# Interleaved halves of the second expert weights in a mixture-of-experts loop

## Chip, cores and metric

The kernel runs on one core of one Trainium2 chip. The metric is device time in microseconds from launch to end; the figure of a kernel is the median of its runs. Before the change that is 1061.54 us (three runs, 1061.35 to 1062.29).

## What is computed

A graph layer and a transformer block work on 625 nodes of 768 features. The graph layer (two attention convolutions over 20,000 edges with self-loops, layer norms, residual products) and the attention with 12 heads take roughly the first 630 us of the span and are not touched. The change is in the last part, a mixture of 8 experts of which each node uses one:

```python
gate_logits = h2 @ Wg                      # h2: layer norm of x, [625, 768]
w, sel = jax.lax.top_k(gate_logits, 1)     # K = 1: the softmax weight is 1
hid = relu(einsum('nd,edf->enf', h2, W1) + b1[:, None, :])   # W1: [8, 768, 3072]
y = einsum('enf,efd->end', hid, W2) + b2[:, None, :]         # W2: [8, 3072, 768]
out = x + (the y of the expert that the node chose)
```

All of it is in float32. An expert's two matrices have 9.4 MB each; they are read from DRAM once for every expert that has nodes.

## The kernel before, in words

**Steps.** The nodes are sorted by expert, and a loop written for the device (L1364) runs over *steps*. A step treats M = 128, 64 or 32 rows of one expert; one branch of the loop body is compiled for each size. One step of 128 rows (A) runs ahead of the loop. In the profiled run the loop's nine steps have 64, 128, 64, 32, 128, 64, 32, 64 and 32 rows. Steps of one expert follow each other without a reload.

**Pieces and halves.** Each matrix lies in SBUF as three pieces: `w1[c]` holds all 768 rows and 1024 columns of the first weights as [128, 6, 1024], `w2[c]` holds 1024 rows of the second weights as eight blocks of 128 rows, [128, 8, 768]. There is one buffer for each piece. `load_piece` (L1034) fills a piece with two DMAs of 1.5 MB on SyncE's queue, a *half* each: for first weights three of the six row blocks, for second weights blocks 0 to 3 and blocks 4 to 7. `w1[2]` has buffers ahead (`load_ahead`, L1081), from which ScalarE copies it (`from_ahead`, L1085), so that this piece is asked for one step sooner.

**Chunks.** `step` (L1088) puts P = 128 / M groups of columns side by side in the array, so that each matmul uses M columns of it. It goes over the hidden features in n chunks. `into(c)` (L1099) multiplies the rows by a chunk of the first weights, `turn(c)` (L1111) transposes the result and applies bias and relu, and `out_of(c)` (L1122) multiplies by the second weights and adds up over all chunks in two PSUM banks (`py[i]`, i the half of the output columns). For M = 128 there are six chunks of 512 hidden features, so chunk c uses one half of piece c // 2. For M = 64 and 32 there are three chunks, each a whole piece; group g of a 64-row chunk works on blocks 4g to 4g + 3, group g of a 32-row chunk on blocks 2g and 2g + 1. K is the number of blocks to a group: 4, 4 and 2. In the trace each float32 matmul is two instructions.

**Order.** Inside a step TensorE's order is written out by hand: the first `into`s, then `turn`s and `out_of`s. `out_of` goes over k (blocks of a group) outside and i inside, in the last chunk over i outside, so that VectorE can add one half of the output (L1184) while the other is computed. SyncE's order is fixed as well (`load_expert`, L1069): `w1[0]`, `w1[1]`, the bias, `w2[0]`, the two buffers ahead, `w2[1]`, `w2[2]`. These loads are issued while the step before still computes, each as soon as the last reader of its destination is done; where the next step has the same expert, they are issued with a false condition and move nothing. GpSimd's queue carries the gathers of rows and the final scatter of each step.

Of the kernel before, what the change touches and what calls it, by code (L numbers as in the profile page):

```python
# [25 lines left out]
KD = D // 128  # L26
# [21 lines left out]
FC = 1024  # L48
# [14 lines left out]
def gnn_moe_kernel(ctx: ExitStack, tc: tile.TileContext, p, out):  # L63
    nc = tc.nc
# [26 lines left out]
    def halves(name, w, k, n):  # L91

        r = k // 2 * 128
        return [wload(f"{name}{i}", k // 2, n,
                      w[i * r:(i + 1) * r, :].rearrange("(k p) n -> p k n", p=128))
                for i in range(2)]
# [51 lines left out]
    with tc.tile_pool(name="gnn", bufs=1) as gp:  # L148
        C = gp.tile([R, T, N], F32, name="C")
# [30 lines left out]
        with tc.tile_pool(name="oneh", bufs=12) as op_, \  # L180
# [15 lines left out]
            w1 = halves("w1", p["L0_gnn_W1"], KD, HC)  # L196
# [253 lines left out]
            with tc.If(ok == 0):  # L450

                nc.vector.memset(C, 0.0)
                for a in range(0, EJ, PART):
                    clear()
                    for q in range(a, a + PART):
                        g, j = q // GJ, q % GJ
                        ohs = step(past[:, g, j:j + 1], True)
                        ohd = target(N, dst[:, g, j:j + 1], upper[:, g, j:j + 1])
                        for t in range(T):
                            nc.tensor.matmul(cps[:, t, :SH + 1], ohd[:, cols(t)], ohs, start=False,  # L460
                                             stop=False, skip_group_check=True)
# [14 lines left out]
        with tc.tile_pool(name="gw", bufs=2, reuse_waits="tile") as gw, \  # L476
# [68 lines left out]
            w2 = halves("w2", p["L0_gnn_W2"], KH, D)  # L545
# [148 lines left out]
    with tc.tile_pool(name="att", bufs=1, reuse_waits="tile") as a1, \  # L694
# [11 lines left out]
        def head_weights(name, w, which=(0, 1)):  # L706
            got = []
            for i in which:
                t_ = wp.tile([128, 3072], F32, tag="w", name=f"{name}{i}")
                v_ = t_[:, :KD * 384].rearrange("p (k n) -> p k n", k=KD)  # L710
                for k in range(KD):
                    nc.sync.dma_start(
                        v_[:, k, :].rearrange("p (h s) -> p h s", h=6),
                        w[6 * i:6 * i + 6, k * 128:(k + 1) * 128, :].rearrange("h p s -> p h s"))
                got.append(v_)
            return got
# [51 lines left out]
        w = head_weights("L0_ffn_Wv", p["L0_ffn_Wv"])  # L768
        for t in range(T):
            for i in range(2):  # L770
                pp = ps.tile([128, 512], F32, tag="p1", name="pv")
                for c in range(KD):
                    nc.tensor.matmul(pp[:R, :384], hT[:, c, cols(t)], w[i][:, c, :],
                                     start=(c == 0), stop=(c == KD - 1))
# [212 lines left out]
        for i in range(len(units) + 2):  # L987
            if i < len(units):
                j, t = units[i]
# [9 lines left out]
            if i >= 2:  # L999
                j, t = units[i - 2]  # L1000
# [22 lines left out]
    W1, W2, b2 = p["L0_ffn_W1"], p["L0_ffn_W2"], p["L0_ffn_b2"]  # L1023
    w1, w2 = [None] * NFC, [None] * NFC
# [8 lines left out]

    def load_piece(e, l, c, **cond):  # L1034
        if l:
            for k in range(0, FC // 128, 4):
                nc.sync.dma_start(  # L1037
                    w2[c][:, k:k + 4, :],
                    W2[ds(e, 1), c * FC + k * 128:c * FC + (k + 4) * 128, :]
                    .rearrange("o (k p) d -> p (o k) d", p=128), **cond)  # L1040
        else:
            for k in range(0, KD, 3):
                load_half(w1[c][:, k:k + 3, :], e, c, k, **cond)
# [44 lines left out]
    def step(M, xT, bT, rb, after=None):  # L1088
# [3 lines left out]
        P = B // M  # L1092
        C = 512 if P == 1 else FC // P
        n = DF // (C * P)
        K = C // 128
        py = [sp.tile([128, 512], F32, name=f"py{i}", bufs=1) for i in range(2)]
        hb, hbT, copied = {}, {}, []

        def into(c):  # L1099
            ph = sp.tile([128, 512], F32, name="ph")  # L1100
            w, o = (w1[c // 2], (c % 2) * C) if P == 1 else (w1[c], 0)
            for k in range(KD):
                for g in range(P):
                    mm = nc.tensor.matmul(ph[g * M:(g + 1) * M, :C], xT[:, k, :M],  # L1104
                                          w[:, k, o + g * C:o + (g + 1) * C],
                                          start=(k == 0), stop=(k == KD - 1))
            hb[c] = mw.tile([128, 512], F32, name="hb")
            copied.append(nc.vector.tensor_copy(hb[c][:, :C], ph[:, :C]))  # L1108
            return mm

        def turn(c):  # L1111

            tp = sp.tile([128, 4, 128], F32, tag="tp", name="tph")
            for k in range(K):
                nc.tensor.transpose(tp[:, k, :], hb[c][:, k * 128:(k + 1) * 128], ident)  # L1115
            hbT[c] = mw.tile([128, 4, 128], F32, name="hbT", bufs=6)
            for k in range(K):
                for g in range(P):
                    f, r = c * P * K + g * K + k, slice(g * M, (g + 1) * M)
                    nc.scalar.activation(hbT[c][:, k, r], tp[:, k, r], AF.Relu, bias=bT[:, f:f + 1])  # L1120

        def out_of(c):  # L1122
            w, o = (w2[c // 2], (c % 2) * K) if P == 1 else (w2[c], 0)

            order = [(k, i) for k in range(K) for i in range(2)]
            for k, i in sorted(order, key=lambda o: o[1]) if c == n - 1 else order:
                for g in range(P):
                    mm = nc.tensor.matmul(  # L1128
                        py[i][g * M:(g + 1) * M, :384], hbT[c][:, k, g * M:(g + 1) * M],
                        w[:, o + g * K + k, i * 384:(i + 1) * 384],  # L1130
                        start=(c == 0 and k == 0), stop=(c == n - 1 and k == K - 1))
            return mm

        with tc.manual_schedule(engines={PE}):
            into(0)
            begun = into(1)
# [42 lines left out]
        w = 384 * P // 4  # L1179
# [30 lines left out]
    for i, n in ((0, T), (1, TA)):  # L1210
        for s in range(n):
            nc.tensor.matmul(pc[:1, i * E:(i + 1) * E], ones[:, :1], oh[:, s, :], start=(s == 0),
                             stop=(s == n - 1))

    def row8(name, *shape, tag=None):
        return ap.tile([1, *shape], F32, name=name, tag=tag or name)
# [18 lines left out]
    key = row8("key", E)  # L1235
# [91 lines left out]
    w = tabf[:, 2, :NS]  # L1327
# [36 lines left out]
    with tc.For_i(0, n_blk, 1, iteration_sync="reg_based") as i:  # L1364
        w = word(i)
# [50 lines left out]
```

## Time and profile before

| What | Value |
|---|---|
| Median of the runs | 1061.54 us |
| The profiled execution's own time | 1062.57 us |
| Its span, first to last instruction | 1060.6 us |
| TensorE busy | 1003.9 us, 95% of the span |
| VectorE, ScalarE, GpSimd busy | 456.6, 366.6, 57.1 us |
| Moved by DMA | 195.90 MB, mean 185 GB/s |
| Mean granted TensorE clock | 0.988 of full speed |
| `out_of` (L1128): 960 matmul instructions | 191.7 us |
| `into` (L1104) in the loop: 864 matmul instructions | 154.5 us |
| Loads of pieces of expert weights: issues on SyncE's queue | 114, 1.5 MB each |

The page lists the busy time of each engine, the span in 40 slices, the chain of work that ended last, and groups of instructions with their mean length and the idle time before them, together with what ended that idle time. A busy matmul is a modelled figure, since matmuls are pipelined; the spacing of their starts tells more than their lengths. In the chain, a step of TensorE, a wait for a DMA or a step of another engine each stand with start and length; what is on it sets the end. A window gives the busy time of each engine in a stretch, then the granted clock (1.00 is full), the share of time that the 16 DMA engines were busy, and what they moved. In the names, `ew` is a buffer of expert weights, `hbT` the turned hidden rows, `ph` and `py` the PSUM tiles of `into` and `out_of`.

### The profile page before, as it was taken

The numbers are of one execution on the slowest core, as the hardware profiler recorded it, in microseconds if no ns is written. First come the engines' busy times: TensorE is split into PE (matmuls) and PEld (weight loads), VectorE is DVE, ScalarE is ACT, GpSimd is POOL, SyncE is SP. The second block draws the span as 40 slices with busy tenths as digits, with TensorE's granted clock in tenths as the row PEclk, the third lists the DMA queues.
The fourth block names the chain that finished last, engine by engine and source line by source line (L and its number), as shares of the span: only waits on it lengthen the run. The fifth ranks groups of instructions, "written<-read, shape, count | busy, mean of one in ns | idle before, by whom it ended". The sixth has DMA issues, their size and how long they took to land. (4 is left out here: it accounts for less than half of the span.)

```text
span 1060.6 us, 15061 instructions
## 1 busy us (share of the span) xinstructions
PE 1003.9 (95%) x4763; PEld 571.8 (54%) x4764; DVE 456.6 (43%) x1307; ACT 366.6 (35%) x835; POOL 57.1 (5%) x97
## 2 busy tenths in 40 slices
PE   6889999999999999999999999998999989999893
PEld 4455466677555556666665655543454434534341
DVE  7886796385284930565546655011101121011212
ACT  6667554362040111444433401113131333034231
POOL 1200100000000010000000112000000000000000
PEclk9999999999999999999999999999999999999997
DMA  9300400300420266999000759333659986899793
GB/s 284 134 1 1 161 31 0 134 1 15 90 44 1 69 156 139 403 392 372 4 1 4 294 174 338 128 141 127 241 214 393 405 309 261 323 399 398 280 404 122
DMA packets 86195, 195.90 MB, mean 185 GB/s; under 512 B 32429, under 2 KB 34100, under 8 KB 86137
## 3 DMA queue, kind: packets, MB, share of 16 engines
q1 hardware_dynamic: 80617, 177.14, 46.3%
q0 software_dynamic: 5440, 17.86, 4.9%
q8 instruction: 32, 0.52, 0.2%
q10 hardware_dynamic: 80, 0.16, 0.1%
q14 instruction: 26, 0.21, 0.1%
HBM read 253.45 MB, written 38.37 MB: 275 GB/s over the span
## 5 line engine op out<-in xcount | busy, mean ns | idle before, releaser
L1128 PE MATMUL py<-ew,hbT 128*64 128x384 f32 (+2 forms) x960 | 191.7, 502 | 10.6 <-DMA ew<-in_L_ffn_W_dram 10.6
L1104 PE MATMUL ph<-ew,xbT 128*32 128x256 f32 (+2 forms) x864 | 154.5, 491 | 5.0 <-DVE bT L1067 3.9
L1128 PEld LDWEIGHTS py<-ew,hbT 128*64 128x64 f32 (+2 forms) x960 | 90.6, 147 | 93.0 <-issue 58.1
L1120 ACT ACTIVATE hbT<-tph,bT 128x64 f32<-128x64 f32 (+2 forms) x240 | 55.2, 332 | 215.4 <-PE tph L1115 148.6
L1104 PEld LDWEIGHTS ph<-ew,xbT 128*32 128x32 f32 (+2 forms) x864 | 61.7, 133 | 87.1 <-issue 78.8
L1184 DVE TENSOR_TENSOR yo<-yo,py 64x192 f32<-64x192 f32 (+2 forms) x80 | 27.6, 378 | 163.0 <-PE py L1128 162.1
L1108 DVE COPY hb<-ph 128x512 f32<-128x512 f32 (+1 forms) x39 | 24.4, 628 | 149.4 <-PE ph L1104 148.5
L530 PE MATMUL agg<-xl,zT 125*125 125x256 f32 (+1 forms) x300 | 79.8, 417 | 1.3 <-ACT zT L519 1.1
L530 PEld LDWEIGHTS agg<-xl,zT 125*125 125x125 f32 x300 | 54.5, 188 | 19.6 <-ACT zT L519 2.6
L357 PE MATMUL pp<-w,yT 128*125 128x512 f32 x120 | 56.8, 613 | 0.0
L232 ACT ACTIVATE step<-iota,past 125x314 f16<-125x314 f16 x120 | 55.9, 549 | 0.0
L630 PE MATMUL ph<-wr,h1T 128*125 128x384 f32 x160 | 52.8, 486 | 0.0
L592 PE MATMUL ph<-w,h1T 128*125 128x384 f32 x160 | 52.4, 486 | 0.0
L839 ACT ACTIVATE e<-e,nm 125x125 f32<-125x125 f32 (+4 forms) x60 | 36.0, 602 | 39.5 <-DVE nm L836 39.5
L249 PE MATMUL cps<-step,oh 125*125 125x314 f16 x181 | 37.0, 307 | 10.5 <-ACT step L232 4.8
L902 PE MATMUL po<-wpj,aT 128*125 128x384 f32 x120 | 44.3, 499 | 1.2 <-DVE nm L836 0.7
L242 DVE TENSOR_SCALAR oh<-iota,drel,upper 125x125 f16<-125x125 f16 x160 | 41.1, 314 | 2.9 <-PE cps L249 2.8
L167 PE MATMUL ph<-wr,yT 128*125 128x512 f32 x96 | 42.1, 593 | 0.1
L592 PEld LDWEIGHTS ph<-w,h1T 128*125 128x125 f32 x160 | 30.0, 188 | 21.2 <-issue 0.5
L836 DVE CUSTOM_DVE_ANT_0 e<-sc,later 125x125 f32<-125x125 f32 (+4 forms) x60 | 30.7, 543 | 24.1 <-PE sc L830 24.0
L630 PEld LDWEIGHTS ph<-wr,h1T 128*125 128x125 f32 x160 | 29.8, 188 | 20.8
L810 PE MATMUL pq<-hT,L_ffn_Wq 128*128 128x313 f32 (+1 forms) x144 | 40.9, 432 | 0.0
(333 smaller groups left out, 1298.4 us busy)
## 6 DMA issues: line engine op xcount, KB each, us to landing
ew<-in_L_ffn_W_dram SPq DMA_DIRECT2D x114, 1536.0 KB
xr<-zt SPq DMA_DIRECT2D x5, 3076.0 KB
xg<-zt SPq DMA_DIRECT2D x5, 3072.0 KB
ahead<-in_L_ffn_W_dram SPq DMA_DIRECT2D x10, 1536.0 KB
xid<-in_L_ffn_W_dram SPq DMA_DIRECT2D x10, 1536.0 KB
w<-in_L_gnn_W_dram SPq DMA_DIRECT2D x4, 1536.0 KB
wr<-in_L_gnn_Wr_dram SPq DMA_DIRECT2D x4, 1536.0 KB
b2b<-in_L_ffn_b_dram SPq DMA_DIRECT2D x11, 384.0 KB
```

The costliest lines, as they stand in the source:

```text
L167: nc.tensor.matmul(pp[:R, :], yT[:, c, cols(t)], part(wr1, KD, c, i, 512), start=(c == 0), stop=(c == KD - 1))
L232: nc.scalar.activation(o, iota[:, :SH + 1], AF.Sign, bias=at, scale=-1.0)
L242: m = nc.vector.tensor_scalar(o, iota[:, :n], at, weight, op0=OP.is_equal, op1=OP.mult)
L357: nc.tensor.matmul(pp[:R, :], yT[:, c, cols(t)], part(w1, KD, c, i, 512), start=(c == 0), stop=(c == KD - 1))
L530: nc.tensor.matmul(self.agg[:R, c0:c0 + n], zT[:, s, :], xl[:, s, x0:x0 + n], start=(s == 0), stop=(s == T - 1))
L592: nc.tensor.matmul(ph[:R, :384], h1T[:, c, cols(t)], part(w2, KH, c, i, 384), start=(c == 0), stop=(c == KH - 1))
L630: nc.tensor.matmul(ph[:R, :384], h1T[:, k, cols(t)], part(wr2, KH, k, i, 384), start=(k == 0), stop=(k == KH - 1))
L810: nc.tensor.matmul(pp[:, :b - a], w[:, c, c0:c0 + 128], hT[:, c, a:b], start=(c == 0), stop=(c == KD - 1))
L902: mm = nc.tensor.matmul(pp[:R, i, :384], aT[:, c, cols(t)], wpj[i][:, c, :], start=(c == 0), stop=(c == KD - 1))
L1104: mm = nc.tensor.matmul(ph[g * M:(g + 1) * M, :C], xT[:, k, :M], w[:, k, o + g * C:o + (g + 1) * C], start=(k == 0), stop=(k == KD - 1))
L1120: nc.scalar.activation(hbT[c][:, k, r], tp[:, k, r], AF.Relu, bias=bT[:, f:f + 1])
L1128: mm = nc.tensor.matmul(py[i][g * M:(g + 1) * M, :384], hbT[c][:, k, g * M:(g + 1) * M], w[:, o + g * K + k, i * 384:(i + 1) * 384], start ...
```

## The change

A half of a piece of the second weights now holds every other block: the first DMA brings blocks 0, 2, 4 and 6, the second 1, 3, 5 and 7. What uses the halves follows:

- In steps of 128 rows chunk c uses the blocks of the same parity as c: block 2k + c % 2. Its columns of the first weights are then four runs of 128, every other block of 128 columns; the product lands in PSUM as one stretch of 512, as before. The bias columns follow.
- In steps of 64 and 32 rows group g keeps its blocks gK + k. `out_of` goes over the k with even blocks first, then those with odd blocks: 0, 2, 1, 3 for 64 rows and 0, 1 for 32 rows. In the last chunk i stays outside.

```diff
     def load_piece(e, l, c, **cond):
         if l:
-            for k in range(0, FC // 128, 4):
-                nc.sync.dma_start(
-                    w2[c][:, k:k + 4, :],
-                    W2[ds(e, 1), c * FC + k * 128:c * FC + (k + 4) * 128, :]
-                    .rearrange("o (k p) d -> p (o k) d", p=128), **cond)
+            of_e = W2[ds(e, 1), c * FC:(c + 1) * FC, :].rearrange(
+                "o (k two p) d -> two p (o k) d", two=2, p=128)
+            to = w2[c].rearrange("p (k two) d -> two p k d", two=2)
+            for i in range(2):
+                nc.sync.dma_start(to[i], of_e[i], **cond)
...
+        def block(c, g, k):
+            return 2 * k + c % 2 if P == 1 else g * K + k
+
         def into(c):
             ph = sp.tile([128, 512], F32, name="ph")
-            w, o = (w1[c // 2], (c % 2) * C) if P == 1 else (w1[c], 0)
+            if P == 1:
+                w = w1[c // 2].rearrange("p k (j two f) -> p k two j f", two=2, f=128)[:, :, None, c % 2]
+            else:
+                w = w1[c].rearrange("p k (g j f) -> p k g j f", g=P, f=128)
             for k in range(KD):
                 for g in range(P):
-                    mm = nc.tensor.matmul(ph[g * M:(g + 1) * M, :C], xT[:, k, :M],
-                                          w[:, k, o + g * C:o + (g + 1) * C],
-                                          start=(k == 0), stop=(k == KD - 1))
+                    mm = nc.tensor.matmul(
+                        ph[g * M:(g + 1) * M, :C].rearrange("p (j f) -> p j f", f=128),
+                        xT[:, k, :M], w[:, k, g], start=(k == 0), stop=(k == KD - 1))
...
-                    f, r = c * P * K + g * K + k, slice(g * M, (g + 1) * M)
+                    f = block(c, g, k) + (c // 2 if P == 1 else c) * (FC // 128)
+                    r = slice(g * M, (g + 1) * M)
...
         def out_of(c):
-            w, o = (w2[c // 2], (c % 2) * K) if P == 1 else (w2[c], 0)
+            w = w2[c // 2 if P == 1 else c]
-            order = [(k, i) for k in range(K) for i in range(2)]
+            order = [(k, i) for k in sorted(range(K), key=lambda k: block(c, 0, k) % 2)
+                     for i in range(2)]
...
-                        w[:, o + g * K + k, i * 384:(i + 1) * 384],
+                        w[:, block(c, g, k), i * 384:(i + 1) * 384],
```

## The prediction

> **What bounds the kernel now.** I read the page first, for the chain that ended last, then the matmul groups with shapes kept apart, to see whose wait is on that chain.
>
> ```profile
> PE 27%; DMA 5%; issue 0%; DVE 0%; POOLq 0%; DVEq 0%; SPq 0%
> ```
>
> ```profile
> L1128 PE MATMUL py<-ew,hbT 128*32 128x384 f32 x288 | 31.6, 536 | 10.6 <-DMA ew<-in_L_ffn_W_dram 10.6
> ```
>
> TensorE is busy nearly throughout. The only transfers it waits for in the expert loop are second weights, 10.6 us, all in the steps of 32 rows (stationary 128x32); the forms of 64 and 128 rows show none. The chain in order of time says when (start, length, what):
>
> ```profile
> 841.69 1.03 PE ph L1104 x16
> ...
> 842.82 19.33 DMA ew<-in_L_ffn_W_dram
> ...
> 862.29 2.77 PE py L1128 x28
> ...
> 1024.12 20.18 DMA ew<-in_L_ffn_W_dram
> ...
> 1044.44 4.49 PE py L1128 x28
> ```
>
> A half piece of 1.57 MB that is issued at 842.82 lands 19.33 us later. At the 406 GB/s of a window below it needs 3.9 us by itself, so the rest is queue. The third stall, at 984, is built alike (issued 965.80, landed 983.86). TensorE's timeline shows where in the last chunk each stall lies (two instructions to a matmul):
>
> ```profile
> 858.63 0.84 PE L1128 MATMUL py<-ew,hbT 128*32 128x384 f32 x4
> 862.29 2.77 PE L1128 MATMUL py<-ew,hbT 128*32 128x384 f32 x28 [2.82 <-DMA ew<-in_L_ffn_W_dram]
> ...
> 984.00 4.31 PE L1128 MATMUL py<-ew,hbT 128*32 128x384 f32 x28 [3.02 <-DMA ew<-in_L_ffn_W_dram]
> ...
> 1044.44 4.47 PE L1128 MATMUL py<-ew,hbT 128*32 128x384 f32 x28 [2.88 <-DMA ew<-in_L_ffn_W_dram]
> ```
>
> Four instructions (row groups 0 and 1, blocks 0 and 2) use the first half, group 2 needs block 4, and 28 wait for the second half.
>
> Next, what would let that half land sooner. SyncE's timeline in the step of 64 rows that loads it, and the windows around the issue (clock, DMA share, GB/s at the end of the line):
>
> ```profile
> 829.80 1.38 SPq L1037 DMA_DIRECT2D ew<-in_L_ffn_W_dram  x2
> ...
> 836.14 7.95 SPq L1037 DMA_DIRECT2D ew<-in_L_ffn_W_dram  x4
> ```
>
> ```profile
> 826.00:828.00 2.00, 2.00 (x16) 0.93 (x14) 0.00 (x0) 2.00 (x8) 0.00 (x0) 1.00 1.04 416
> 828.00:830.00 2.00, 2.00 (x16) 0.86 (x13) 0.00 (x0) 0.48 (x3) 0.00 (x0) 1.00 1.02 406
> 830.00:832.00 2.00, 2.00 (x17) 1.12 (x17) 0.00 (x0) 1.64 (x9) 0.00 (x0) 1.00 1.03 412
> ```
>
> The engines are full before, at and after the moment at which the release (chunk 0 ends at 829.68) lets SyncE go on. The share over 786 to 862 is 0.99, over 910 to 984 1.01, over 998 to 1043 0.99. Adding up the issues since 786.6 (eleven halves of 1.57 MB, about 1 MB of bias and row loads: 18.3 MB) and what the windows moved by 830 (16.9 MB) leaves 1.4 MB queued, 3.4 us. At 1010.67, the same point of the last load, four halves were issued (6.3 MB) and 4.3 moved: 5 us queued.
>
> **The change, part by part.** (1) *Earlier release in steps of 64 rows.* In chunks 0 and 1 the even blocks (k = 0, 2) now come first, so the even half is free after 16 of 32 instructions: 5.31/2 = 2.65 us earlier, at 827.0 for 829.7. SyncE may issue that much earlier; queued behind it there are the odd half, the loads ahead and the other two pieces, which follow as before or sooner. But 3.4 and 5 us of transfers stand in front: the DMA engines take the half up no earlier. Worth 0. If the cover were gone it would be worth up to 2.65 us at each of three stalls.
>
> (2) *Order in steps of 32 rows.* In the last chunk k = 0 uses blocks 0, 2, 4, 6, all even. So eight instructions instead of four precede the wait; behind it on TensorE stand 24, then VectorE's adds and the scatter. One costs 2.77/32 to 2.79/32, 0.087 us (row at 855.54: x32 in 2.79): 4 x 0.087 = 0.35 us less behind each landing. The first half does land in time for all eight: it goes through the queue 3.9 us earlier (the x4 ran without a wait at 858.63). In chunk 1 of the last step (a wait of 1.13 us) the gain is swallowed by the wait of chunk 2.
>
> (3) *How the 0.35s add.* After 862 the next step, 128 rows, is TensorE's own, and its releases from 903.5 on start the next full stretch of DMA: the landing at 983.86 comes 0.35 earlier. The one after hangs on the loads ahead issued just behind that landing (first weights wait at 996.43 for them) and again on a full queue, so the second 0.35 is lost while the first is passed on: landing 1043.96 for 1044.31. Then 24 instead of 28: 0.35 more. Sum so far -0.70.
>
> (4) *The clock behind the last stall.* The x28 took 4.47 there and 2.77 at 862, because the granted clock was halved:
>
> ```profile
> 984.00:986.00 2.00, 2.00 (x16) 0.77 (x20) 0.00 (x0) 0.00 (x0) 0.00 (x0) 0.50 0.00 0
> ...
> 1044.00:1046.00 2.00, 1.56 (x16) 0.79 (x20) 0.00 (x0) 0.00 (x0) 0.00 (x0) 0.79 0.04 8
> 1046.00:1048.00 2.00, 2.00 (x14) 0.76 (x8) 1.35 (x3) 0.00 (x0) 0.00 (x0) 0.50 0.00 0
> ```
>
> 0.79 over two microseconds is half speed from 1045.16. Stalls of 3.02 and 2.88 cooled, one of 2.82 didn't. The new last stall runs from eight instructions behind the first half (1040.38 + 1.19 = 1041.57) to 1044.09: 2.5 us. The Trainium skill ("TensorE: Matmul & The Clock Gate", section "Why this matters for your kernels") asks for no idle gaps above about 3 us. By it 2.5 us stays warm and all 1.70 us of the slow part goes: -2.4 in all. The rows disagree with it already at 2.88, and the drop came 0.7 us after work had resumed, so it looks like a slot of time more than a length of gap. If it falls at 1045.16 again, 1.07 us or 12 instructions run fast and 12 slowly (2.08): the end is at 1047.2 for 1048.9, -1.7 in all. If the timed runs never cool there, the gain is -0.7. I take -1.3, between the three. The other cooled stall, at 984, gives nothing: what follows it is paced by transfers.
>
> (5) *Full steps read first weights in four runs of 128 columns, 1 KB apart.* 216 instructions in three steps, 0.43 us apart (5.15/12), 93 us, all on the path. No row has such a moving operand. Nearest: L274 loads 125 columns 16 bytes apart, 303 to 326 ns; the contiguous load of 128 took 338 at half clock and 190 at full, and the clock at L274 reads full, so that row would warn; but it lies in the first 6 us, uses the weight port and reads single words. Upper end: four separate reads of 128 (transposes: four in 0.44) against 0.43, +2.2 us. Lower end 0[...]. I take 0: a run of 512 bytes has one jump in 128 words and is nearer to the contiguous row than to the one that jumps at every word.
>
> (6) *The half as a transfer.* Same count (66 issues), bytes and 3072-byte rows; the block step in DRAM doubles from 384 to 768 KB, the destination is no longer one stretch. A rule of the Trainium skill speaks against that ("DMA: Bandwidth & Descriptors", section "Latency and other measured facts"): copies whose partitions lie a large power of two apart in DRAM[...] ran at half the rate or less. Partitions here stay 3 KB apart; if the step between blocks counted like it, the 28 halves on the three full stretches (28 x 3.9 = 109 us) could cost another 109. The row decides against it: first weights step 1.5 MB from block to block and ran at 418 and 422 GB/s (990 to 994), second weights with 384 KB at 402 to 416. I take 0, bounds 1% either way: 1.1 us.
>
> (7) *Cost nothing:* k order 0, 2, 1, 3 (ScalarE wrote block 2 a whole chunk, 5.3 us, before it is read; without that cover 0.4 us per chunk); bias columns renumbered; halves of full steps are still a chunk each. Same instruction counts.
>
> Sum: profiled execution 1062.57 (span 1060.6 and 1.97 around it) - 1.3 = 1061.27. It lay 1.03 above the median of 1061.54, so the median goes to 1060.2.
>
> **Rivals.** *A, only the order counts:* 1060.2; chance 0.72. *B, the release moves the transfers:* each landing 2.65 earlier on top: -3.0 at the first stall, -3.0 more at the second, up to -3 at the third with its clock: 1052.5. For it: SyncE's longest waits are for just this release; against it the full windows. Chance 0.07. *C, slower, waits by range:* if a half's dependencies are kept over its whole extent, two interleaved halves count as overlapping. Then in a full step the first half of second weights waits for both chunks (780.7 becomes 786), the full DMA stretch starts a half (3.9 us) short, at 862 and again at 984, and no instruction of the last chunk precedes the last half (8 x 0.087 = 0.7): +3.9 +3.9 +0.7, 1070. It decides as soon as one such false wait exists. The trace shows that waits follow slices (first weights' half issued at 810.78 inside chunk 0, which ends at 812.6), though no interleaved ones: 0.07. *D, the runs cost:* +2.2 less 1.3: 1062.4; it decides above 1.4% of 93 us; 0.14.
>
> **Numbers.** 0.2% is 2.1 us, about what a measurement of this kernel can tell from no change. Faster by more: B, and A with the clock by the skill's rule or a slightly quicker transfer: 0.07 + 0.13 = 0.20. Slower by more: C, and D with a slower transfer: 0.07 + 0.05 = 0.12. The rest 0.68. The range covers A with its clock and transfer bounds, and most of D: 1058.7 to 1062.3.
>
> **What would show it.** x8 ahead of the wait and x24 behind it in the three last chunks; SyncE's issues 2.65 us earlier and longer in the queue (19.3 becoming 22) with landings moved by at most 0.4; PEclk in the final 6 us; matmuls of full steps still 5.15 us per 12; DMA at 402. Wrong if a landing moves by over 1 us, if a half waits for the other's chunk, or if the full steps' rows lengthen.

## The result and the profile after

The changed kernel takes 1058.12 us (median of 20 runs, 1054.71 to 1062.41), the kernel before 1062.34 in the same session (20 runs, 1058.05 to 1065.66): a ratio of 0.9962, interval 0.9951 to 0.9973. That is some 4 us less where 1.3 were forecast, and 0.6 us below the lower end of the range. The profiled execution took 1056.86 us with a span of 1054.9 and a mean granted clock of 0.990.

The group of second-layer matmuls in steps of 32 rows, with shapes kept apart, stood at 31.6 us busy and 10.6 us of idle time before; after the change:

```profile
L1138 PE MATMUL py<-ew,hbT 128*32 128x384 f32 x288 | 27.8, 523 | 7.0 <-DMA ew<-in_L_ffn_W_dram 7.0
```

The idle time is smaller mostly because the first of the three stalls (2.82 us before) is gone in this execution: the first 32-row step started 5 us late (below), by which time its weights had come. The other two are there, in TensorE's timeline:

```profile
977.41 0.85 PE L1138 MATMUL py<-ew,hbT 128*32 128x384 f32 x8
981.27 3.07 PE L1138 MATMUL py<-ew,hbT 128*32 128x384 f32 x24 [3.01 <-DMA ew<-in_L_ffn_W_dram]
984.27 6.09 PE L1112 MATMUL ph<-ew,xbT 128*64 128x512 f32 x24
...
1035.86 0.85 PE L1138 MATMUL py<-ew,hbT 128*32 128x384 f32 x8 [1.01 <-DMA ew<-in_L_ffn_W_dram]
1039.70 3.46 PE L1138 MATMUL py<-ew,hbT 128*32 128x384 f32 x24 [2.99 <-DMA ew<-in_L_ffn_W_dram]
```

Eight instructions ahead of the wait and 24 behind it, as planned. SyncE's timeline for the 64-row step that loads these weights shows the earlier release: the first half of `w2[0]` is issued 19.9 us behind the start of the step (at 803.20), where it was 22.4 before (829.80 behind 807.37), and the last group 26.2 us behind it, where it was 28.8.

```profile
823.09 2.95 SPq L1041 DMA_DIRECT2D ew<-in_L_ffn_W_dram  x2
826.83 0.09 SPq L1031 DMA_DIRECT2D ahead<-in_L_ffn_W_dram  x1
827.57 0.08 SPq L1031 DMA_DIRECT2D xid<-in_L_ffn_W_dram  x1
829.43 3.96 SPq L1041 DMA_DIRECT2D ew<-in_L_ffn_W_dram  x2
```

The full steps kept their pace (the chain of waits: twelve first-layer instructions in 5.15 us, as before), and so did the transfers (the windows over the two full stretches: clock, share, GB/s at the end of the line; before, 388 with share 1.01 over 910 to 984).

```profile
873.30 5.15 PE ph L1112 x12
```

```profile
908.00:981.00 73.00, 70.27 (x480) 32.74 (x478) 9.69 (x28) 22.99 (x58) 4.18 (x6) 1.00 1.01 393
1000.00:1038.00 38.00, 35.70 (x346) 16.09 (x342) 6.64 (x17) 19.34 (x48) 2.04 (x3) 1.00 1.02 396
```

Where the time went is read by marks that all executions have: the start of the first 64-row step in the loop, the start of the second one, the landings (TensorE goes on with the last chunk) in the second and the last 32-row step, and the end of that chunk. Two executions of the kernel before and three of the changed one (its own, e2 and, as told below, e9):

| Stretch, us | before | changed | difference of means |
|---|---|---|---|
| first to second 64-row step | 106.2, 106.0 | 102.8, 104.9, 104.2 | -2.2 |
| second 64-row step to landing 2 | 176.6, 178.5 | 178.1, 178.2, 177.4 | +0.3 |
| landing 2 to landing 3 | 60.4, 59.7 | 58.4, 58.4, 58.2 | -1.7 |
| landing 3 to the last matmul | 4.5, 4.2 | 3.5, 3.4, 3.3 | -1.0 |
| sum | 347.8, 348.5 | 342.7, 344.9, 343.0 | -4.6 |

The sum is about what the timed runs show. The forecast had 0, -0.35, 0 and -0.95 in these rows. Two rows need care. All three changed executions have a gap of some 5 us ahead of the first 32-row step (below), of the two before only the second; beside that one alone the second row is -0.6, so the 0.35 forecast there can be neither seen nor ruled out. And in the first row these few executions flatter the change: between the eleven profiles with the early release and the five without it is -1.3.

### The profile page after: what moved, and what is told of

It reads as the page before. It is cut to its first block, busy times and chain, and to the rows that moved or that the text cites. A ratio compares the mean times of both kernels' runs of the same rounds, so it can differ in the third digit from the quotient of the medians.

```text
span 1054.9 us, 15062 instructions
## 1 busy us (share of the span) xinstructions
PE 999.0 (95%) x4763; PEld 572.7 (54%) x4764; DVE 456.3 (43%) x1307; ACT 366.4 (35%) x835; POOL 57.0 (5%) x97
## 5 line engine op out<-in xcount | busy, mean ns | idle before, releaser
L1138 PE MATMUL py<-ew,hbT 128*64 128x384 f32 (+2 forms) x960 | 187.8, 499 | 7.0 <-DMA ew<-in_L_ffn_W_dram 7.0
L1112 PEld LDWEIGHTS ph<-ew,xbT 128*32 128x32 f32 (+2 forms) x864 | 64.2, 135 | 89.0 <-issue 82.4
L249 PE MATMUL cps<-step,oh 125*125 125x314 f16 x181 | 37.1, 307 | 10.5 <-ACT step L232 6.9
```

Of the source, the lines that this page charges most:

```text
L1112: mm = nc.tensor.matmul(ph[g * M:(g + 1) * M, :C].rearrange("p (j f) -> p j f", f=128), xT[:, k, :M], w[:, k, g], start=(k == 0), stop=(k ...
L1138: mm = nc.tensor.matmul(py[i][g * M:(g + 1) * M, :384], hbT[c][:, k, g * M:(g + 1) * M], w[:, block(c, g, k), i * 384:(i + 1) * 384], star ...
```

## Experiments

Ratios are to the kernel before, run on the same chip in the same session, with 95% intervals. Medians of one kernel wander by 1 to 2 us from session to session, so a difference of less than 0.15% between two kernels is a hint only.

| Run | Median, us | Ratio |
|---|---|---|
| e1 before, again | 1061.75 | 0.9998 [0.9988, 1.0009] |
| e2 changed, again | 1056.92 | 0.9957 [0.9943, 0.9970] |
| e3 release late | 1060.03 | 0.9974 [0.9964, 0.9985] |
| e4 odd block first | 1060.89 | 0.9991 [0.9981, 1.0001] |
| e5 release only | 1061.03 | 0.9989 [0.9977, 1.0000] |
| e6 16 ahead, 16 behind | 1056.80 | 0.9949 [0.9932, 0.9967] |
| e7 changed, busy in the wait | 1057.03 | 0.9952 [0.9932, 0.9972] |
| e8 before, busy in the wait | 1061.51 | 0.9982 [0.9965, 0.9999] |
| e9 rows written later | 1057.43 | 0.9958 [0.9940, 0.9975] |
| e10 one more issue | 1054.91 | 0.9939 [0.9917, 0.9960] |
| e11 16 and 16, busy | 1055.40 | 0.9943 [0.9923, 0.9962] |
| e12 rows held | 1056.85 | 0.9958 [0.9941, 0.9974] |
| e13 before, rows early | 1061.28 | 0.9995 [0.9982, 1.0008] |
| e14 changed, rows early | 1059.79 | 0.9974 [0.9954, 0.9994] |

**The two kernels once more.** No edit.

> The kernel before, unchanged, for a second profile of it: which of its stalls cool the clock, and how long each stage takes, when the execution is another one. Theory of order and clock: the stretch from the landing at the end of the 32-row step before (983.86 in the first profile) to the last landing (1044.31) is 60.4 us again, within 0.5, since it is paced by transfers. Theory that the first profile was slow there by chance (row loads that trickled between 996 and 1004): about 58.5 us, as in the profile of the changed kernel. Time equal to the kernel before.

> The changed kernel, unchanged, for a second profile of it. The gap of 4.96 us ahead of the first 32-row step (842.47) was in none of the stalls of before: if the change causes it, it stands here again; if it is chance, it is gone and the step starts at once. Last two landings 58.4 us apart if the release moves the last loads by 2 us, anything between 58 and 60.5 if chance. Time 0.996 of the kernel before.

The gain repeats. Between the last two landings e1 has 59.7 us, near the first profile's 60.4 and far from 58.5, and e2 has 58.4 again. Both executions also show a gap of 4.8 us with no releaser but "issue" ahead of the first 32-row step. So do the changed kernel's own profile and ten of the fourteen experiments (e8 and e13, variants of the kernel before, among them), while the first profile of before has none. With it, the stall of that step is absent, but the stretch from that 64-row step to the next full step takes 59.3 us in e1, against 57.6 in the first profile of before. The gap comes with either kernel and is no part of the change; its neighbours in the trace are transfers of instructions.

**Release and order taken apart.** e3 is the changed kernel whose 64-row steps use the blocks in the order 0, 1, 3, 2, so that an even half stays in use nearly to the end of its chunk:

```diff
-            order = [(k, i) for k in sorted(range(K), key=lambda k: block(c, 0, k) % 2)
-                     for i in range(2)]
+            ks = [0, 1, 3, 2] if P == 2 else sorted(range(K), key=lambda k: block(c, 0, k) % 2)
+            order = [(k, i) for k in ks for i in range(2)]
...
```

> The changed kernel, but steps of 64 rows go over k = 0, 1, 3, 2: an even block is read last, so that the even half comes free at the end of a chunk, as in the kernel before, and 2.65 us later than in the changed one. Theory that the DMA engines are full there (the prediction): SyncE's issue is 2.65 us later, no landing moves by more than 0.4 us and the time is that of the changed kernel, within 1 us. Theory that the earlier release moves the transfers: the landings in the three 32-row steps come 1 to 2.7 us later with respect to the start of the 64-row step that issues them, and the time is 2 to 4 us above the changed kernel.

e4 is the changed kernel that uses the odd blocks first in the last chunk of 32-row steps so that all 32 instructions lie behind the wait:

```diff
...
+            ks = ks[::-1] if P == 4 and c == n - 1 else ks
...
```

> The changed kernel, but in the last chunk of 32-row steps the odd block (the half that lands last) is used first: 32 instructions stand behind the landing instead of 24 and none ahead of it. The release in 64-row steps is as in the changed kernel. Theory of order: 8 x 0.087 = 0.7 us more at the first stall and at the last, 1.4 us in all, and the stalls are longer (3.7 us where 3.0 stood), so that the clock cools more surely: up to 1.7 us more at the end. 1.4 to 3 us above the changed kernel. Theory of release: the order is worth nothing beyond noise, time as the changed kernel within 0.7 us.

e5 keeps the release and gives that chunk the old order, four instructions ahead and 28 behind:

```diff
...
+            if P == 4 and c == n - 1:
+                todo = todo[:2] + todo[4:8] + todo[2:4] + todo[8:]
...
```

> The changed kernel with its layout and its early release in 64-row steps, but in the last chunk of 32-row steps two matmuls (four instructions) use the even half, then come those on the odd half: 28 instructions stand behind the landing, as in the kernel before. Theory of order and clock (what the change gains lies in the 32-row steps, and in what their earlier end moves): time of the kernel before, within 0.8 us; from the resumption in the second last 32-row step to the next step about 4.2 us, from there to the last resumption about 60 us. Theory of release: 1.5 us below the kernel before, and the last landing follows that of the step before by 58.5 us although 28 instructions stand behind it.

e4 loses most of the gain, e5 about 3 of the 4 us. So the order is the larger part, and it is worth more than the 0.087 us an instruction that it was costed at. At full clock the rows of these kernels have 4 instructions in 0.84 us and 8 in 0.85, 20 in 2.13 (e10) and 24 in 2.14 (e7), 28 in 2.77 and 32 in 2.79: a begun eight (four groups, two instructions each) takes as long as a full one. Leaving 24 behind the wait instead of 28 therefore saves 2.77 - 2.14 = 0.63 us, not 0.35. TensorE's timeline of e5, second and last 32-row step:

```profile
981.92 4.44 PE L1143 MATMUL py<-ew,hbT 128*32 128x384 f32 x28 [3.02 <-DMA ew<-in_L_ffn_W_dram]
...
1042.49 5.35 PE L1143 MATMUL py<-ew,hbT 128*32 128x384 f32 x28 [2.97 <-DMA ew<-in_L_ffn_W_dram]
```

28 instructions, all or in part at half clock, cost 4.4 to 5.4 us, against 3.1 and 3.5 for the 24 of the changed kernel, and from landing to landing it is 60.6 us, as before the change. The release, on the other hand, isn't worth nothing: e3 lies some 1.8 us above e2 and e5 1.2 below the kernel before (each at the edge of its uncertainty). It does not act through the transfers of a full stretch: from the start of the third 64-row step to the landing behind it (landing 2) it takes 53.2 to 53.9 us in e1 to e5 alike, released early or late. It acts at the turn of the loop behind the first 64-row step. The loads of pieces are issued with a false condition there, and only the two buffers ahead are filled (3.05 MB between 727 and 736 us in the profile of before). TensorE's timeline there, before, changed, e3 and e5 (the last two lines end with their windows, hence fewer instructions):

```profile
739.34 13.24 PE L1104 MATMUL ph<-ew,xbT 128*128 128x512 f32 x24 [3.89 <-DVE bT L1067]
```

```profile
737.87 10.54 PE L1112 MATMUL ph<-ew,xbT 128*128 128x512 f32 x24 [3.13 <-DVE bT L1068]
```

```profile
738.45 7.08 PE L1112 MATMUL ph<-ew,xbT 128*128 128x512 f32 x12 [3.83 <-DVE bT L1068]
```

```profile
738.57 6.67 PE L1112 MATMUL ph<-ew,xbT 128*128 128x512 f32 x15 [3.10 <-DVE bT L1068]
```

The gap is 3.9 us before and 3.1 changed; e3, which takes the early release away, has 3.8, and e5, which has nothing but the release, 3.1. (The releaser named, the copy of the bias, starts 2.7 us behind the last matmul in every kernel, so it is not what differs.) Over the profiles the gap is 2.8 to 3.5 us with early release and 3.6 to 3.9 without (before, e1, e3, e8, e13), without overlap. Behind it the clock can drop: 24 instructions of the full step took 10.5 us in the changed kernel, its full pace, and 13.2 before. The granted clock at the same time in both (before, then changed) is the third figure from the end of the line:

```profile
743.00:745.00 2.00, 2.00 (x4) 0.86 (x3) 0.00 (x0) 0.00 (x0) 0.00 (x0) 0.55 0.78 286
```

```profile
743.00:745.00 2.00, 2.00 (x6) 0.94 (x5) 0.69 (x1) 0.00 (x0) 0.00 (x0) 1.00 0.65 240
```

That pace was kept in three of the eleven profiles with early release and in none of the five without, which can be chance: the other eight have 12.0 to 13.5 us, the five 12.2 to 13.2. From the first to the second 64-row step it makes 104.3 us in the mean (102.8 to 105.8) against 105.7 (105.0 to 106.2): -1.3 us, near what e3 and e5 say. The gap is about half of it (3.15 against 3.77 us in the mean), the clock the rest.

**Where the second landing goes.** In the changed kernel the 64-row step between the landings starts sooner, and the second landing comes sooner with it. e6 puts 16 instructions ahead of the wait by leaving k outside in that chunk:

```diff
-            for k, i in sorted(order, key=lambda o: o[1]) if c == n - 1 else order:
+            for k, i in (sorted(order, key=lambda o: o[1]) if c == n - 1 and P != 4 else order):
```

> The changed kernel, but the last chunk of 32-row steps runs with k outside too, so that 16 instructions use the even half ahead of the wait and 16 stand behind it. Theory of order and clock: 8 x 0.087 = 0.7 us less behind each landing, stalls of 2.3 us where 3.0 stood, and with them a clock that stays up; the 64-row step starts 1.5 us after the resumption where 3.0 stood, its row loads fall into the gap of the transfers and the last landing follows 57.5 us after the one before (58.4 in the changed kernel). The last adds of VectorE, 8 of 0.57, then set the end. 1 to 2.5 us below the changed kernel. Theory of release: as the changed kernel, within 0.7 us.

e6 ran its 16 instructions behind landing 2 in 1.58 us, but then the clock fell all the same (48 first-layer instructions in 13.4 us instead of 10.5). The landings are 58.7 us apart, not 57.5, the last 16 instructions took 2.23 us, and in time it is 0.8 us below the change (e2).

e7 keeps the change and gives TensorE three more matmuls ahead of the wait, whose result nobody reads; e8 does the same to the kernel before.

```diff
...
+                    if P == 4 and c == n - 1 and done == 4:
+                        for _ in range(3):
+                            nc.tensor.matmul(idle[:, :384], hbT[c][:, 0, :], w[:, 0, :384],
+                                             start=True, stop=True)
+                    done += 1
...
```

> The changed kernel with three matmuls more into an unused PSUM tile (results not used) between the instructions on the even half and the wait for the odd half, in the last chunk of 32-row steps: 3 x 0.65 = 1.9 us of work inside a stall of 3.0. Theory of the clock: it is not lowered behind these stalls, the 24 instructions take 2.1 us where 3.0 to 3.5 stood, the next step starts 2.2 us after the resumption, the last landing follows 57.5 us after the one before, and the end comes 1.3 us sooner behind it: 1.5 to 2.5 us below the changed kernel, less up to 1.9 us at the first 32-row step where the execution has no wait there. Theory that the clock follows the clock slot alone: no change but the cost, up to 1.9 us above.

> The kernel before with the same three matmuls (results not used) ahead of the wait in the last chunk of 32-row steps. Theory of order and clock: the 28 instructions take 2.4 us where 4.2 to 4.5 stood, the 64-row step starts sooner behind the landing and the last landing follows after 58 us instead of 59.7 to 60.4: 2 to 3.5 us below the kernel before, less up to 1.9 us at the first 32-row step: most of what the change gains, without the change. Theory of release: the clock gives 1.7 us at the end at most, the landing stays at 60 us.

In e7 the clock stays up, and 24 instructions take 2.14 us behind both landings:

```profile
982.75 2.14 PE L1146 MATMUL py<-ew,hbT 128*32 128x384 f32 x24 [0.59 <-DMA ew<-in_L_ffn_W_dram]
984.98 6.23 PE L1112 MATMUL ph<-ew,xbT 128*64 128x512 f32 x28
...
1040.42 2.14 PE L1146 MATMUL py<-ew,hbT 128*32 128x384 f32 x24 [0.86 <-DMA ew<-in_L_ffn_W_dram]
```

From landing to landing it is now 57.7 us: a start of the step that is 0.8 us sooner than in the changed kernel brought the next landing 0.8 us nearer. In the kernel before, e8 brought the start 1.4 us nearer and the landing 0.8 (59.3 us). In time e7 gained 0.5 us on e2 and e8 1.9 us on the kernel before, less than the 1.5 to 2.5 and 2 to 3.5 expected; the three matmuls cost up to 1.9 us at the first 32-row step where that has no stall. The landings moved, so the forecast's full queue isn't there. The windows of the kernel before in the 64-row step show it (share and GB/s last):

```profile
994.00:996.00 2.00, 2.00 (x12) 0.59 (x10) 0.43 (x1) 0.00 (x0) 0.56 (x1) 1.00 0.89 356
996.00:998.00 2.00, 2.00 (x12) 0.71 (x10) 0.00 (x0) 0.00 (x0) 0.53 (x1) 1.00 0.72 207
998.00:1000.00 2.00, 2.00 (x12) 0.76 (x10) 0.69 (x1) 0.48 (x3) 0.00 (x0) 1.00 0.69 212
1000.00:1002.00 2.00, 2.00 (x12) 0.67 (x10) 0.00 (x0) 1.27 (x7) 0.00 (x0) 1.00 0.96 293
1002.00:1004.00 2.00, 2.00 (x12) 0.62 (x10) 0.00 (x0) 1.70 (x1) 0.00 (x0) 1.00 1.02 301
```

and of the changed one, at about the same distances from its landing 2 (10 us and more):

```profile
992.00:994.00 2.00, 2.00 (x12) 0.61 (x10) 0.00 (x0) 0.00 (x0) 0.54 (x1) 1.00 1.00 401
994.00:996.00 2.00, 2.00 (x12) 0.70 (x8) 0.41 (x1) 0.00 (x0) 0.00 (x0) 1.00 0.78 160
996.00:998.00 2.00, 2.00 (x11) 0.77 (x12) 0.28 (x1) 1.73 (x8) 0.00 (x0) 1.00 0.94 367
998.00:1000.00 2.00, 2.00 (x12) 0.63 (x10) 0.00 (x0) 0.97 (x2) 0.00 (x0) 1.00 1.02 414
```

The queue runs dry some 11.5 us behind a landing, and the first packet of the next first weights comes 13.1 to 14.2 us behind it, in all sixteen profiles and however soon the step starts. What differs is the stretch after that: eight or nine slow microseconds before, some three changed. Reckoned at 414 GB/s, the 13 us from 11 us behind the landing lose 3.3 to 3.6 us in the kernel before and 1.5 to 1.6 in the changed one. That difference is as large as the 1.7 us between the landings. In the slow stretch lie the gathers of rows that GpSimd issues at the start of the step: changed, their packets end 13.9 us behind the landing, as the stream begins; before, they trickle in until 18.8 (e1) and 20.4.

**Do the gathers set it?** e9 wrote the gather of `rb` further down in the code; it was still issued at the same place (11.2 us behind the landing, 11.1 in the changed kernel), so this run is the change once more and tells nothing of the question.

```diff
...
+            with tc.issue_after(begun.ins):
+                rows()
...
```

> The changed kernel, with the gather of a step's running sums (rb, rows of 3076 bytes) issued only behind the second half of the first layer of its step instead of ahead of it; nothing else differs. Theory A (the landing that ends the kernel is late or early with these row gathers, which find the queue idle if they come within 11 us of the landing before, and disturb the stream of weights if they come later): the stretch from the resumption in the second 32-row step to that in the last one grows from 58.4 us to 60 or more, and the time by 1.5 to 2 us, to a ratio of 0.9972 to 0.9982. Theory B (the landing follows the loads ahead and the release alone): the stretch stays at 58.4, the ratio at 0.9955 to 0.9965.

e12 makes it wait for TensorE:

```diff
...
+            begun = next(step)
+            with tc.issue_after(begun.ins):
+                tc.add_manual_dep(rows().ins, begun.ins.name, ORDER)
...
```

> The changed kernel, with the gather of a step's running sums (rb) made to wait for the second half of the first layer's instructions on TensorE, so that it is issued some 10.5 us behind the start of its step instead of 8. (The run before with this aim only wrote the gather further down; the trace shows it issued at the same place, so it was the change once more.) Theory A (row gathers that come into the stream of first weights slow it, and those that come ahead of it do not): the rows of the 64-row step fall behind 14 us after the landing, the stream runs at some 300 GB/s for 3 to 5 us, and from the resumption in the second 32-row step to that in the last one it takes 59.5 to 60.5 us instead of 58.4; the ratio rises to 0.9972 to 0.9982. Theory B (the stretch follows the start of the 64-row step for another reason, such as when SyncE comes to issue): 58.2 to 58.6 us, ratio 0.9955 to 0.9965.

e13 and e14 let ScalarE issue it and read the row number for it, in the kernel before and in the changed one:

```diff
-        nc.gpsimd.dma_start(rb[:M], xr[ds(row, M), :])
+        nc.scalar.dma_start(rb[:M], xr[ds(row, M), :])
...
```

> The kernel before, with the gather of the running sums issued by ScalarE at the start of a step instead of by GpSimd, which comes to it only behind the scatter of the step ahead and the gather of xb. Theory A (late row gathers slow the stream of first weights): the rows of the 64-row step come ahead of the first weights, the stretch between the resumptions falls from 60.2 us to 58.6 to 59.2, and the ratio is 0.9985 to 0.9990. Theory B: 59.7 to 60.5 us, ratio 1.000, or above it by what ScalarE's register loads and the issue cost ahead of its first activation.

> The changed kernel with the same move of the gather to ScalarE. Theory A: its rows came ahead of the stream already, so there is little to gain: 58.0 to 58.5 us between the resumptions, ratio 0.9950 to 0.9965. Theory B: the same 58.4 us. Both differ from the kernel before with this move, where theory A expects a gain and theory B none.

What GpSimd issues, in its timeline of e12:

```profile
990.14 0.93 POOL L1195 DMA_INDIRECT out_dram<-yo,idx  x1 [17.90 <-DVE yo L1193]
992.98 0.56 POOL L1382 DMA_DIRECT2D xb<-xg  x1 [1.92 <-PE ph L1111]
997.01 0.53 POOL L1389 DMA_DIRECT2D rb<-xr  x1 [3.46 <-PE tph L1122]
```

Its landing 2 was at 983.62, so the gather came 13.4 us behind it, and its rows took 7.7 us to land where they took 3.6 in the changed kernel. The stream lost 2.8 us instead of 1.5. But from landing to landing it is 58.5 us, as in the changed kernel: this execution lost only 2.2 us in the rest of the way (from 24 us behind landing 2), where the three of the changed kernel lost 3.1 to 3.3. Beside e3 and e7, whose 64-row step also starts 2.2 us behind landing 2, it is 0.8 to 0.9 us more. In the time the late rows aren't seen: 0.9958, as e9, where theory A expected 0.9972 or more.

The sixteen profiles together are clearer than any one of them. Between the two landings 20.6 MB move in each, 49.8 us at 414 GB/s, so the distance is this and what the queue loses. SyncE issues the next first weights 12.1 to 13.2 us behind landing 2 in all of them. The gather of `rb` comes with its step or, in e12 to e14, as edited, and the profiles fall into two groups by it, with nothing between:

| Gather issued behind landing 2 | Profiles | Gathers' packets end | Lost from 11 to 24 us | Landing to landing, mean |
|---|---|---|---|---|
| 8.6 to 11.2 us | changed, e2, e3, e6, e7, e9, e10, e11, e14; e8, e13 | 13.3 to 14.2 us | 1.3 to 1.9 us | 58.2 us (57.5 to 59.3) |
| 12.5 to 13.5 us | before, e1; e4, e5, e12 | 18.8 to 20.4 us | 2.7 to 3.6 us | 59.7 us (58.5 to 60.6) |

Each group has variants of both kernels, and e12, which differs from e9 only in holding this gather, carries the changed kernel's stretch from one to the other (1.5 us lost in e9, 2.8 in e12). So a step that starts 1.2 us sooner brings its gathers ahead of the stream (11.1 us instead of 12.5), and the 1.9 us which the stream then doesn't lose cover the 1.7. That the landing itself follows is not shown by an edit: what the queue loses behind 24 us differs by 2 us from profile to profile (2.2 to 4.2) for a reason that no run here shows. It is why e12 has no more than 58.5, and e8, with early rows, 59.3 (4.1 us lost there).

In time e13 (0.9995) seems to show no gain. But 4.5 us of its timed runs lie outside the span (median), against 2.7 in the kernel before in the same session. The spans are 1057.1 us against 1059.1, more than the 1.1 to 1.6 that theory A expected. e14 has 4.2 us outside and a span of 1055.2, that of the change (1055.0 in e2, 1055.5 in e9): no gain, as theory A expects where the rows are early anyway. The spans hold the whole program, so they don't say in which stretch e13 gained; and why the move to ScalarE costs time outside the span is open.

**What shortens the turn of the loop?** e10 loads the last odd half by two DMAs, so that SyncE again has two issues left behind the last matmul:

```diff
             for i in range(2):
-                nc.sync.dma_start(to[i], of_e[i], **cond)
+                if i and c == NFC - 1:
+                    nc.sync.dma_start(to[i][:, :2], of_e[i][:, :2], **cond)
+                    nc.sync.dma_start(to[i][:, 2:], of_e[i][:, 2:], **cond)
+                else:
+                    nc.sync.dma_start(to[i], of_e[i], **cond)
```

> The changed kernel, with the last odd half of the second weights (the one whose space comes free with the last instruction of a step) loaded by two DMAs of two blocks each instead of one of four, so that SyncE has two issues left behind the last instruction of a step, as in the kernel before. Theory A (the gap between the first 64-row step and the full step behind it is set by what SyncE has left to do there): the first instruction of the full step comes 3.75 to 3.9 us behind the end of the last second-layer instruction instead of 3.1 to 3.5, the full step takes 67 to 68 us instead of 66.4 in the mean, and the time grows by 1 to 1.5 us, to a ratio of 0.9970 to 0.9975. Theory B (the gap differs for another reason, such as the order of the last instructions on TensorE): the gap stays at 3.1 to 3.5 us and the ratio at 0.9955 to 0.9965.

Theory A of this run falls: SyncE's last issue ended 0.90 us behind the last matmul (0.91 before, 0.24 changed), and the gap was still 3.1 us. What goes with the gap in every profile is the moment at which a transfer of instructions starts: 1.0 to 1.5 us ahead of the end of the last matmul with early release, 0.5 to 0.9 without. SyncE gets past its wait for the even half sooner, so it could be the code behind that wait which is asked for earlier. Or it is the two buffers ahead: they too are issued 0.7 us or more sooner, and their last packets end 0.8 to 1.4 us ahead of the last matmul's end with early release, 0.2 to 0.4 without (e13 and e14 left out, whose gather moves at that time). No run here varies one of these by itself. e10 came out no slower than the change for another reason as well. Its split wait keeps TensorE at work inside the stall:

```profile
982.42 0.84 PE L1142 MATMUL py<-ew,hbT 128*32 128x384 f32 x4 [0.78 <-DMA ew<-in_L_ffn_W_dram]
984.32 2.13 PE L1142 MATMUL py<-ew,hbT 128*32 128x384 f32 x20 [1.06 <-DMA ew<-in_L_ffn_W_dram]
```

**Both parts together.** e11 has e6's edit and e7's, with the three matmuls (their result unread again) behind 16 instructions; the cut is against e7:

```diff
-                    if P == 4 and c == n - 1 and done == 4:
+                    if P == 4 and c == n - 1 and done == 16:
```

> The changed kernel with 16 instructions ahead of the wait and 16 behind it in the last chunk of 32-row steps, and three more matmuls ahead of the wait whose result nobody reads. Theory A (what lies behind a landing costs its instructions at full clock if TensorE was kept busy, and an earlier start of the 64-row step brings the next landing forward): x16 in 1.43 us behind both landings, 57.0 to 57.8 us between them, a ratio of 0.9940 to 0.9948, ahead of the change and of either of its two parts alone. Theory B (the order is worth only its instructions, the clock nothing in the timed runs): 0.995 to 0.996.

It ran 16 instructions in 1.50 us behind both landings, with 58.0 us between them. It is clearly faster than the kernel before. The four kernels that leave less behind the wait or keep the clock up (e6, e7, e10, e11) lie at 0.9939 to 0.9952, the three runs of the change itself (with e9) and e12 at 0.9957 to 0.9962: all on one side, by 0.5 to 2.4 us, though no single interval separates them.

**Which stalls cool the clock?** Not simply the long ones: 2.82 us (before, at 862) kept it, and so did 2.69 and 2.70 at landing 2 in e3 and e14, while 2.67 there in e9 and 2.27 at the last landing in e6 lost it. In all sixteen traces the granted clock changes only at times that lie a whole number of 3.413 us apart (before: 983.73, 987.15, 1045.17, 1048.59). In slots of that length, the stalls of before at 862 and at 984 look like this (length, TensorE busy; the clock third from the end):

```profile
857.44:860.85 3.41, 2.03 (x18) 0.47 (x10) 0.00 (x0) 1.26 (x3) 0.00 (x0) 1.00 0.80 310
860.85:864.27 3.42, 1.98 (x26) 1.00 (x28) 0.45 (x1) 0.00 (x0) 0.00 (x0) 1.00 0.03 10
864.27:867.68 3.41, 3.41 (x15) 1.35 (x10) 3.21 (x7) 0.00 (x0) 0.00 (x0) 1.00 0.60 166
...
980.32:983.73 3.41, 0.66 (x4) 0.00 (x0) 0.00 (x0) 1.27 (x3) 0.00 (x0) 1.00 0.77 302
983.73:987.15 3.42, 3.15 (x20) 1.15 (x24) 0.34 (x1) 0.00 (x0) 0.00 (x0) 0.50 0.06 5
```

The stall at 862 is split, 1.4 us of idle time to each slot; of the one at 984, 2.75 us fall into one slot, and the next ran at half clock. From 640 us on, the sixteen traces have 1786 slots at full clock. All 53 with more than 2.0 us idle were followed by half clock, none of the 1723 with less than 1.75, and 5 of the 10 between. Where a stall falls in its slot differs from execution to execution, so whether a stall of 2 to 3 us cools the clock is largely luck in these kernels.

## The prediction, step by step

- **Step 1, the earlier release: right for the transfers, wrong as a zero.** SyncE issued 2.5 us sooner and the landings behind 64-row steps stayed, as argued. But the step looked only at the stretches in which second weights move. Where their loads have a false condition, the same release shortened the turn of the loop from 3.9 to 3.1 us, and in the mean the clock behind it was lost for less time: about 1.2 to 1.8 us by e5 and e3, which the forecast had at 0. By what path it shortens the turn is open.
- **Step 2, the order: right in place, mis-sized.** x8 ahead, x24 behind, at both stalls that this execution has. The price of 4 x 0.087 = 0.35 us shared the time of 32 instructions out evenly; they go in eights, and it is 0.63 us at full clock (28 in 2.77, 24 in 2.14).
- **Step 3, how the 0.35s add: wrong, and with step 1 the reason for the miss.** It said that the landing after the one at 984 "hangs on the loads ahead" and "on a full queue", so that a gain there is lost. The second landing came 1.7 us nearer to the one before it: a landing that moves by over 1 us was the prediction's own sign of being wrong. The queue is empty for some 2 us early in that stretch in every profile. The evidence was in the trace of before: the windows from 994 to 1000, with shares of 0.89, 0.72 and 0.69, lie in just that stretch, and the forecast's 0.99 over 998 to 1043 begins behind two of them and averages the third away. Late gathers of rows cost the stream there 1.3 us in e12; before and changed differ by 1.9 us in it. How much of that reaches the landing is not shown by an edit.
- **Step 4, the clock: right in sum at the end by luck, wrong at 984.** From the last landing to the last matmul it gained 1.0 us, against 0.35 + 0.6 forecast. But the stall was not 2.5 us: the first half landed late as well (x8 waited 1.01 us), so it was 2.99, and it cooled. The sum came out because an eight at half clock is worth more than 0.35 us (28 in 5.3 us in e5 and e13, 24 in 4.07 in e3 and e12). The guess that the drop follows "a slot of time more than a length of gap" was right. The Trainium skill's 3 us ("TensorE: Matmul & The Clock Gate", section "Why this matters for your kernels") is no safe limit here, since stalls of 2.67 us (e9) and 2.27 us (e6) cooled. "The other cooled stall at 984 gives nothing" is step 3's error again: there the gain was 1.2 us to the start of the next step, and the landing behind it came sooner.
- **Steps 5 and 6, strided first weights and the half's layout: right.** 5.15 us for twelve instructions, 393 and 396 GB/s. The clock of the row at L274 was not known, though: the trace's record of it begins at 17.8 us. And the bound of 109 us was too high: the Trainium skill ("DMA: Bandwidth & Descriptors", section "Latency and other measured facts") has 207 GB/s at a pitch of 512 KiB where the full rate is 214, and half the rate only at 4 and 8 MiB. No slowing shows here with blocks 768 KB and partitions 3 KB apart.
- **Step 7: right.** No new wait by range, no new wait of ScalarE.
- **Rivals.** B, C and D are refuted by the rows above. A had much of the mechanism (order and clock), but its price, 1.3 us, was some 3 too small: it left out the turn of the loop (1.3 us) and the second landing (1.7 us).

## What to carry over

An average share of 0.99 over a stretch says nothing about the two microseconds in which the queue runs dry; before a gain is written off as hidden by transfers, look at the windows right behind the landing that starts it. Here the instructions behind a wait of 3 us were paid at half clock and, it seems, once more at the next landing through the row gathers that they held back: move such instructions ahead of the wait, and count them in the units in which they run (here eights). And ask of a release that moves what it does in iterations in which no piece is loaded.

## What was not expected of the hardware

- 64 rows of 3076 bytes took 3.6 us to land ahead of a stream of weights and 7.7 to 8.7 inside it, and the stream ran at 212 to 301 GB/s meanwhile instead of 414 (changed and before; e12 for the 7.7).
- The granted clock changes on a grid of 3.413 us, and in these traces a slot with over 2.0 us of idle time was always followed by half clock, one with under 1.75 us never.
- The same turn of the loop took 4.8 to 5.0 us in some executions, ahead of the first 32-row step, and no gap at all in others, with the same kernel (before and e1).
